# Summing the states of a Mamba scan on the four 64x64 tiles of TensorE

## The chip, the cores and the metric

One core of one Trainium2 chip runs the whole kernel in one launch. The metric is the device time in microseconds of one execution. Before the change it is 7373.88 us, the median of three runs (7371.5 to 7379.04).

## The reference, cut to what matters

The input x is (2, 256, 64, 64) in f32, seen as two sequences of 4096 tokens with 256 channels. Layer 0 is a group norm and a Mamba block with 256 inner channels. Layer 1 is a layer norm, a forward and a backward Mamba block with 512 inner channels each, and then a mixture of eight experts of three 256x256 layers. All five scan jobs share this recurrence over 16 states s, for every inner channel d and time t:

```
h[t,d,s] = exp(dt[t,d] * A[d,s]) * h[t-1,d,s] + dt[t,d] * xc[t,d] * B[t,s]
y[t,d]   = sum over s of h[t,d,s] * C[t,s]  +  xc[t,d] * D[d]
out      = (y * silu(z)) @ W_out
```

xc is a causal convolution of four taps of one half of the input projection, put through SiLU; z is the other half; dt is a softplus of a projection of xc; B and C are projections of xc too.

## The kernel before, in words

Channels lie on the 128 partitions and time on the free axis, in chunks of T = 512. Six jobs (layer 0, layer 1 forward and backward, for two batches) of eight chunks give 48 steps. A step has two blocks of 128 channels in layer 0 and four in layer 1. Blocks are taken in pairs (jp), so a layer-0 step has one pair and a layer-1 step two, 80 pairs in all. For each pair the 16 states are taken two at a time: a "quad" (i, jp, n) is two states by two blocks, 8 quads per pair (QN), 640 in all.

What a quad does, with the functions and lines that the change and the prediction's steps touch:

- SyncE loads the rows of B and of C for its two states, copied over all partitions (`load_bc`, L485 to L489). `want` and `flush` (L491 to L497) keep one list of loads for both kinds, in order; a load whose chunk has no B and C yet holds up those behind it.
- GpSimdE (POOL) multiplies dt * xc by B into a buffer bq, 128x2048 (`emit_b`, L504 to L516). There are six such buffers. At n = 0 it first makes xdt = dt * xc (L509).
- ScalarE (ACT) writes the decay exp(dt * A) into PSUM (`emit_decay`, L518), 128x512 at a time. There are two such PSUM tiles, each for one state and two blocks.
- VectorE (DVE) scans (`emit_scan`, L529), 128x512 at a time, four times per quad. In quads with even n the scan writes into bq, in those with odd n into the decay's tile.
- The product with C: for even n it is one POOL instruction of 128x2048 (`emit_times_c_quad`, L559), after a small ACT copy of the last column has saved the carry of the scan (`emit_carry`, L551). For odd n it is a DVE instruction of 128x1024 for each state, with a small DVE copy for the carry (`emit_times_c`, L541).
- TensorE (PE) sums over the states in PSUM by multiplying with an identity (`emit_sum`, L565): for each state and block one f32 matmul of a 128x128 identity with 128x512 of bq, into `y[:, j, :]`. The sum opens with a diagonal matmul for the D skip (`emit_skip`, L574). There is one y tile, of two PSUM banks. `emit_gate` (L583) on DVE multiplies y with silu(z), after which the next pair's skip can begin.

The order of the work around this is written by hand. For every step a `Slots` table holds the side work by slot and queue ("sp", "pe", "act", "dve", "pool"): `prepare` (L337) puts in the next step's projections xs and z, convolution, x_proj, softplus and gate, `norm` (L235) the layer norm, `finish` (L587) the output projection of the step before. A slot is one state of one quad; the main loop (L676 to L727) runs each slot's side work per queue and the slot's own work between it. In it, L693 to L704 say when a quad is summed, and L717 to L722 that POOL gets, in every other quad, the C product of the quad before and then two B products, for two and three quads ahead. The Tile framework then orders the instructions by its own scheduler within each engine, and adds the semaphores.

After the scans a second part computes the experts (L743 to L880). It isn't touched.

## Time and profile before

| | |
|---|---|
| median of three runs | 7373.88 us |
| profiled execution | 7371.24 us |
| its span, first to last instruction | 7369.5 us |
| mean granted TensorE clock | 0.909 |
| busy: PE / DVE / ACT / POOL | 6102.4 / 4677.5 / 3559.7 / 4535.2 us |
| sum over states, L569 (PE) | 5120 matmul instructions, 2363.6 us busy |
| B products, L511 (POOL) | 640 of 4523 ns |
| C products, L560 (POOL) | 320 of 4524 ns |
| C products, L546 (DVE) | 640 of 1218 ns |
| scans, L535 (DVE) | 2560 of 1207 to 1280 ns |
| table loads (ACT) | 416 of 1283 ns |

The profile shows one execution. Busy time is the time in which an engine has an instruction running. PE is the multiplying part of TensorE and PEld its weight loading, which lies beside it; an f32 matmul appears as two of each. For every wait, the profile names the engine and line that released it. A row of groups has the line, engine, operation, output and inputs, shapes, count, busy time, mean duration in ns, and after the bar the idle time just before them and what ended most of it. A row of a timeline has start, duration, engine, line and operation, and in brackets the idle time before it; several alike in a row are merged (x4). A row of the waits has who waited for whom, the total in us, how many times, and the longest.

### The profile page before, as it was taken

How to read it: one execution, taken by the hardware profiler on the slowest of the kernel's cores; microseconds unless marked ns; L12 is line 12 of the kernel's file. 1: busy time of each engine (PE TensorE's matmuls, PEld its weight loads, DVE VectorE, ACT ScalarE, POOL GpSimd, SP SyncE). 2: the span in 40 equal slices, each digit the busy share in tenths (PEclk: the TensorE clock that was granted, in tenths of full speed). 3: DMA queues.
4: the chain of work that ended last, by engine and by line, in shares of the span. 5: the costliest groups of instructions: out<-in, count | busy, mean ns of one | idle time of the engine just before them, and what ended most of it. 6: DMA issues, size and time to landing. Idle time of an engine off the chain costs nothing.

```text
span 7369.5 us, 43337 instructions
## 1 busy us (share of the span) xinstructions
PE 6102.4 (83%) x13160; PEld 2613.7 (35%) x13160; DVE 4677.5 (63%) x4889; ACT 3559.7 (48%) x5295; POOL 4535.2 (62%) x1062
## 2 busy tenths in 40 slices
PE   6888778878787888877777778777776999999999
PEld 2333333333333333333333333333333444444444
DVE  6889877778877877877787777787784111111111
ACT  7887556455445555544544544544542222222222
POOL 6889878878878878877887887887883000000000
PEclk8999989999999999988989889888887999999999
DMA  5444434434433443443343343343332000000000
GB/s 187 147 155 167 157 132 158 143 132 140 144 128 132 146 138 129 146 143 129 129 143 124 132 140 123 126 145 125 128 132 94 8 4 12 12 12 12 12 1 11
DMA packets 254189, 806.30 MB, mean 109 GB/s; under 512 B 26362, under 2 KB 35330, under 8 KB 253954
## 3 DMA queue, kind: packets, MB, share of 16 engines
q1 hardware_dynamic: 253954, 803.53, 32.6%
q8 instruction: 103, 1.69, 0.1%
q14 instruction: 132, 1.08, 0.0%
HBM read 749.95 MB, written 53.48 MB: 109 GB/s over the span
## 4 chain that ended last, share of the span: by engine, by line
POOL 27%; PE 22%; issue 16%; DVE 2%; ACT 1%; DMA 1%; POOLq 0%; SPq 0%; DVEq 0%; ACTq 0%
POOL bq L511 19%; PE hp L835 13%; POOL bq L560 7%; PE ym L869 6%; PE wb L860 1%; POOL xdt L509 1%; PE lg L805 1%; PE var_m L125 1%; DVE bq L535 1%; DVE da L535 1%; PE ym L855 0%; DMA t_dram<-xr 0%; ACT L108 0%; DVE cen_m L118 0%; DMA xr<-t_dram 0%
## 5 line engine op out<-in xcount | busy, mean ns | idle before, releaser
L511 POOL TENSOR_TENSOR bq<-xdt,bc 128x2048 f32<-128x2048 f32 x640 | 2880.7, 4523 | 555.0 <-PE y L569 553.4
L524 ACT ACTIVATE da<-dt,w_a 128x512 f32<-128x512 f32 x2564 | 1751.9, 689 | 1965.6 <-DVE h_state L549 1010.4
L569 PE MATMUL y<-bq,ident 128*128 128x512 f32 x5120 | 2363.6, 608 | 88.1 <-POOL bq L560 51.2
L535 DVE TENSOR_TENSOR_SCAN bq<-da,h_state,bq 128x512 f32<-128x512 f32 x1120 | 1360.0, 1267 | 631.9 <-POOL bq L511 605.2
L560 POOL TENSOR_TENSOR bq<-bq,bc 128x2048 f32<-128x2048 f32 x320 | 1447.6, 4524 | 311.8 <-ACT h_state L555 305.8
L569 PEld LDWEIGHTS y<-bq,ident 128*128 128x128 f32 x5120 | 1002.4, 197 | 1397.3 <-issue 1262.0
L535 DVE TENSOR_TENSOR_SCAN da<-da,h_state,bq 128x512 f32<-128x512 f32 x1120 | 1410.7, 1280 | 61.2 <-ACT da L524 31.4
L839 ACT ACTIVATE h<-hp,of,sc 128x512 f32<-128x512 f32 x512 | 398.4, 778 | 1024.1 <-PE hp L835 1024.1
L361 PE MATMUL conv<-xs,w_conv 128*128 128x512 f32 x1280 | 681.0, 682 | 249.0 <-ACT xs L351 248.1
L546 DVE TENSOR_TENSOR bq<-da,bc 128x1024 f32<-128x1024 f32 x640 | 778.8, 1218 | 12.7
L578 PE MATMUL y<-xc,w_d 128*128 128x512 f32 x320 | 275.0, 1009 | 541.2 <-DVE sz L585 541.2
L866 DVE TENSOR_TENSOR h<-h,wbs 128x1024 f32<-128x1024 f32 x128 | 156.9, 1226 | 874.7 <-ACT h L839 874.7
L361 PEld LDWEIGHTS conv<-xs,w_conv 128*128 128x128 f32 x1280 | 273.8, 219 | 641.5 <-issue 333.8
L835 PE MATMUL hp<-n,W 128*128 128x512 f32 x1024 | 490.4, 633 | 0.0
L835 PE MATMUL hp<-h,W 128*128 128x512 f32 x1024 | 449.9, 592 | 0.0
L869 PE MATMUL ym<-h,Wo 128*128 128x512 f32 x1024 | 449.9, 592 | 0.0
L326 PE MATMUL z<-nx,w_in 128*128 128x512 f32 x640 | 321.6, 635 | 133.4 <-DVE sz L444 76.7
L578 PEld LDWEIGHTS y<-xc,w_d 128*128 128x128 f32 x320 | 88.7, 303 | 680.5 <-DVE sz L585 599.7
L326 PE MATMUL xs<-nx,w_in 128*128 128x512 f32 x640 | 302.5, 604 | 15.0 <-DVE sz L444 5.9
L600 PE MATMUL o<-sz,w_out 128*128 128x512 f32 x640 | 311.9, 624 | 1.1 <-DVE sz L444 0.8
L835 PEld LDWEIGHTS hp<-n,W 128*128 128x128 f32 x1024 | 200.9, 202 | 293.4 <-issue 293.4
L509 POOL TENSOR_TENSOR xdt<-dt,xc 128x1024 f32<-128x1024 f32 x80 | 188.4, 2355 | 187.8 <-DVE dt L423 165.1
(121 smaller groups left out, 4424.2 us busy)
## 6 DMA issues: line engine op xcount, KB each, us to landing
bc<-bcd SPq DMA_DIRECT2D x1280, 512.0 KB, 3.9
t_dram<-xr SPq DMA_DIRECT2D x48, 512.0 KB, 3.6
x<-t_dram SPq DMA_DIRECT2D x32, 512.0 KB, 5.7
xr<-t_dram SPq DMA_DIRECT2D x32, 512.0 KB, 5.2
x<-in_x SPq DMA_DIRECT2D x16, 512.0 KB, 5.1
xr<-in_x SPq DMA_DIRECT2D x16, 512.0 KB, 3.8
t_dram<-x SPq DMA_DIRECT2D x16, 512.0 KB, 3.1
n_dram<-nx SPq DMA_DIRECT2D x16, 512.0 KB, 4.0
```

The source lines that it names most:

```text
L326: nc.tensor.matmul(ps, job.w["in"][:, k, m * P : (m + 1) * P], rhs, start=(k == 0), stop=(k == KC - 1),)
L361: nc.tensor.matmul(v["ps"], w["conv"][:, j, k, :], job.xs[:, j, k : k + T], start=(k == 0), stop=(k == 3),)
L511: nc.gpsimd.tensor_tensor(bq[g], ck["xdt", jp].rearrange("p (o j) t -> p o j t", o=1).to_broadcast([P, 2, 2, T]), bt.pop(g).rearrange("p s ...
L524: nc.scalar.activation(da[g, s][:, j, :], cks[i]["dt", jp][:, j, :], AF.Exp, scale=steps[i][0].w["a"][:, 2 * jp + j, 2 * n + s : 2 * n + s ...
L535: nc.vector.tensor_tensor_scan(d[:, j, :] if n % 2 else b, d[:, j, :], b, job.h[:, 2 * n + s, 2 * jp + j : 2 * jp + j + 1] if c else 0.0, ...
L546: nc.vector.tensor_tensor(bq[g][:, s, :, :], d, ct[g][:, s : s + 1, :].to_broadcast([P, 2, T]), ALU.mult)
L560: nc.gpsimd.tensor_tensor(bq[g], bq[g], ct[g].rearrange("p s (o t) -> p s o t", o=1).to_broadcast([P, 2, 2, T]), ALU.mult,)
L569: nc.tensor.matmul(y[i, jp][:, j, :], ident, bq[g][:, s, j, :], start=False, stop=(n == QN - 2 and s == 1),)
L578: nc.tensor.matmul(y[i, jp][:, j, :], job.w["d"][:, 2 * jp + j, :], cks[i]["xc", jp][:, j, :], start=True, stop=False,)
L835: nc.tensor.matmul(ps, w[:, k, m * P : (m + 1) * P], x[:, k, :], start=(k == 0), stop=(k == KC - 1),)
L839: nc.scalar.activation(h[:, m, :], ps, AF.Relu, bias=of[:, l, e, m : m + 1], scale=sc[:, l, e, m : m + 1],)
L869: nc.tensor.matmul(y[:, b, m, :], we["Wo", e][:, k, m * P : (m + 1) * P], h2[b][:, k, :], start=False, stop=(e == E - 1 and k == KC - 1),)
```

## The change

`emit_sum` and `emit_skip` no longer multiply with the full 128x128 array. They issue four matmuls instead of two, each with a 64x64 piece of the (diagonal) weight: the tile (r, col) takes rows 64r to 64r+63 of block j = (col - r) mod 2, and writes to partitions 64col to 64col+63 of bank r of y. So y holds the two blocks in another arrangement of channels than before. The host arranges the z columns of W_in and the rows of W_out alike (`summed`, `z_last`), so that gate and output projection fit.

The products with C on POOL are those of quads 0, 2, 3 and 5 instead of 0, 2, 4 and 6 (`POOL_C`, with the quad at which each is summed). The last quad of a pair is therefore one of DVE's. `POOL_AT` writes out at which quad POOL gets which C product (c) and B product (b). Loads of B and of C have a list each. DVE's side work runs between the two scans of a slot instead of before them. The layer norm's steps from the square on come one slot later, and in layer 1 the preparation of the next step starts at slot 4 instead of 5.

```diff
+TILES = [(r, col, (col - r) % 2) for r, col in ((0, 0), (1, 1), (0, 1), (1, 0))]
+POOL_C = {0: 2, 2: 4, 3: 5, 5: 7}
+POOL_AT = {0: "b3", 1: "c0 b4 b5", 3: "c2 b6", 4: "c3 b7", 6: "c5 b8 b9", 7: "b10"}
...
-                (0, "pe", mean), (1, "dve", centre), (1, "act", square), (2, "pe", variance),
-                (3, "act", roots), (4, "dve", divide), (4, "pool", add), (5, "act", affine),
-                (6, "sp", store),
+                (0, "pe", mean), (1, "dve", centre), (2, "act", square), (3, "pe", variance),
+                (4, "act", roots), (5, "dve", divide), (6, "pool", add), (6, "act", affine),
+                (7, "sp", store),
...
-                s0 += 5 if steps[i + 1][0].layer and not steps[i + 1][0].flip else 1
+                s0 += 6 if steps[i + 1][0].layer and not steps[i + 1][0].flip else 1
...
-        loads, wanted = [], []
+        loads, wanted = ([], []), []
...
         def want(h, *gs):
-            loads.extend((h, g) for g in gs if g < nq)
+            loads[h].extend(g for g in gs if g < nq)
 
         def flush():
-            while loads and "bc" in cks[quads[loads[0][1]][0]]:
-                h, g = loads.pop(0)
-                load_bc(g, h, ct if h else bt)
+            for h in range(2):
+                while loads[h] and "bc" in cks[quads[loads[h][0]][0]]:
+                    load_bc(loads[h].pop(0), h, ct if h else bt)
...
-        def emit_scan(g, s):
+        def emit_scan(g, s, j):
...
-            for j in range(2):
-                b = bq[g][:, s, j, :]
-                nc.vector.tensor_tensor_scan(
-                    d[:, j, :] if n % 2 else b, d[:, j, :], b,
...
+            b = bq[g][:, s, j, :]
+            nc.vector.tensor_tensor_scan(
+                b if n in POOL_C else d[:, j, :], d[:, j, :], b,
...
         def emit_sum(g, ss):
             i, jp, n = quads[g]
             for s in ss:
-                for j in range(2):
+                for r, col, j in TILES:
+                    rows, out_ = slice(64 * r, 64 * r + 64), slice(64 * col, 64 * col + 64)
                     nc.tensor.matmul(
-                        y[i, jp][:, j, :], ident, bq[g][:, s, j, :], start=False,
-                        stop=(n == QN - 2 and s == 1),
+                        y[i, jp][out_, r, :], ident[rows, rows], bq[g][rows, s, j, :],
+                        start=False, stop=(n == QN - 1 and s == 1),
                     )
...
-            for j in range(2):
+            for r, col, j in TILES:
+                rows, out_ = slice(64 * r, 64 * r + 64), slice(64 * col, 64 * col + 64)
                 nc.tensor.matmul(
-                    y[i, jp][:, j, :], job.w["d"][:, 2 * jp + j, :], cks[i]["xc", jp][:, j, :],
-                    start=True, stop=False,
+                    y[i, jp][out_, r, :], job.w["d"][rows, 2 * jp + j, rows],
+                    cks[i]["xc", jp][rows, j, :], start=True, stop=False,
                 )
...
-        want(0, 3, 4)
+        want(0, 3, 4, 5)
...
-                prepare(i + 1, 5 if wide else 0, sl, 1 if wide or steps[i + 1][0].nj == 2 else 2)
+                prepare(i + 1, 4 if wide else 0, sl, 1 if wide or steps[i + 1][0].nj == 2 else 2)
...
-                    sl.run(slot, "dve")
...
                     if s == 0:
-                        if n % 2 == 0:
-                            if g >= 1:
-                                emit_sum(g - 1, (1,))
-                            if g >= 2:
-                                emit_sum(g - 2, (0, 1))
...
-                    elif n % 2:
+                        if g and (n - 1) % QN not in POOL_C:
+                            emit_sum(g - 1, (1,))
+                        for m, due in POOL_C.items():
+                            if due == n:
+                                emit_sum(g - n + m, (0, 1))
+                    elif n not in POOL_C:
                         emit_sum(g, (0,))
...
-                    if s == 0 and n % 2:
+                    if s == 0 and n - 1 in POOL_C:
                         emit_carry(g - 1)
...
-                    if s == 0 and n % 2:
-                        emit_times_c_quad(g - 1)
-                        want_b(g + 2, g + 3)
-                        want(1, g + 1, g + 2)
-                        want(0, g + 4, g + 5)
+                    if s == 0:
+                        for what in POOL_AT.get(n, "").split():
+                            m = g - n + int(what[1:])
+                            if what[0] == "c":
+                                emit_times_c_quad(m)
+                            else:
+                                want(0, m + 3)
+                                flush()
+                                want_b(m)
+                    else:
+                        want(1, g + 2)
                         flush()
                     sl.run(slot, "pool")
 
-                    emit_scan(g, s)
-                    if n % 2:
+                    emit_scan(g, s, 0)
+                    sl.run(slot, "dve")
+                    emit_scan(g, s, 1)
+                    if n not in POOL_C:
                         emit_times_c(g, s)
...
+    def summed(din):
+        o = np.empty(din, np.int64)
+        for jp in range(din // (2 * P)):
+            for r, col, j in TILES:
+                at, of = (2 * jp + r) * P + 64 * col, (2 * jp + j) * P + 64 * r
+                o[at : at + 64] = np.arange(of, of + 64)
+        return o
+
+    def z_last(w):
+        din = w.shape[1] // 2
+        return np.concatenate([w[:, :din], w[:, din:][:, summed(din)]], axis=1)
```

## The prediction

> **What bounds the kernel now.** I read the windows first, to split the span, then the waits of the scan part, the timelines of two engines over one stall, and the groups.
>
> The window table (columns PE, weight loads, DVE, ACT, POOL busy, then clock and DMA), for the part with 512 inner channels and for the part after the scans:
>
> ```profile
> 1190.00:5605.00 4415.00, 3499.29 (x7374) 1484.98 (x7375) 3448.94 (x3566) 2216.43 (x3468) 3567.41 (x831) 0.90 0.40 134
> 5605.00:7369.50 1764.50, 1642.81 (x3756) 728.12 (x3754) 268.33 (x290) 487.07 (x612) 0.00 (x0) 0.92 0.04 14
> ```
>
> In the scan part three engines are each busy for 78 to 81%: none is full, they wait for each other. The change touches nothing in the last 1764.5 us (93% TensorE). The part before 1190 (L0, 16 pairs of blocks) has POOL at 965.0 of 1138 us. The waits of 1190 to 5605:
>
> ```profile
> DVE bq L535 <- POOL bq L511: 647.4, 232, 7.5
> ...
> POOL bq L511 <- PE y L569: 553.4, 85, 10.1
> ...
> POOL bq L560 <- ACT h_state L555: 270.9, 186, 5.2
> ...
> DVE xc L375 <- ACT thx L371: 201.5, 92, 3.3
> ```
>
> The scans wait for POOL's B product, and POOL's B product waits for TensorE to have summed the quad whose buffer it takes (six buffers bq). All 553.4 us of that wait of the whole run lie here. One such stall, on POOL and then on PE:
>
> ```profile
> 3028.21 8.98 POOL L511 TENSOR_TENSOR bq<-xdt,bc 128x2048 f32<-128x2048 f32 x2 [7.63 <-PE y L569]
> ```
>
> ```profile
> 3022.81 1.88 PE L569 MATMUL y<-bq,ident 128*128 128x512 f32 x4
> 3024.53 1.88 PE L326 MATMUL xs<-nx,w_in 128*128 128x512 f32 x4
> 3026.24 5.31 PE L569 MATMUL y<-bq,ident 128*128 128x512 f32 x12
> 3031.39 3.60 PE L361 MATMUL conv<-xs,w_conv 128*128 128x512 f32 x8
> ```
>
> PE is not waiting here: it works off a queue without a gap, and the sum that frees the buffer is in its turn at 3026. So TensorE binds where a chunk's projections and convolutions fall, and the cost lands on POOL, then on DVE. How much of TensorE the sums are:
>
> ```profile
> L569 PE MATMUL y<-bq,ident 128*128 128x512 f32 x5120 | 2363.6, 608 | 88.1 <-POOL bq L560 51.2
> ```
>
> 5120 instructions for 640 x 2 x 2 = 2560 calls: an f32 matmul is two load-and-multiply passes, and in the timeline passes start 0.43 us apart (12 in 5.31 with the last lasting 0.59).
>
> **What the Trainium skill says.** "TensorEngine Tiling (Array Packing)", Key Properties: tiles work independently and may load and multiply in parallel, and a change of tiling mode drains TensorE. The trace of before has no 64x64 form, but it has a mode change, priced below. Same page, Restrictions and Gotchas: different row tiles must not use one PSUM bank at a time; the change writes row half r to bank r of y, so this rule is kept (no run here shows the price of breaking it). "TensorE: Matmul & The Clock Gate", Part 3, Measured speedup: sixteen 32x32 tiles gave 10.6 times; whether in f32 is not said, and no run here shows it. Same part, The mechanism: matmuls start and end in program order; before agrees as far as it goes, one tile's passes follow each other at 0.43 us.
>
> **The change, part by part.**
>
> *Sums and skip.* 2560 + 160 calls become 5120 + 320, each with a 64x64 weight and all 512 columns, so each pass streams as long as now, 0.43 us. One state of a quad is 4 tile calls, 8 passes. Four tiles at once: two rounds, 0.86 us. Now: 2 calls, 4 passes, 1.72 us. So full overlap halves 2363.6 to 1182 us, one running at a time doubles it to 4727; I take full overlap because the skill states independence and a measured gain, and keep both ends. Weight loads double to 8 per state: the trace has two loads in 0.29 us with 0.18 for one, so 0.11 apart, 8 x 0.11 = 0.85 us, just under 0.86 if a 64-column load costs as much as one of 128. It should not bind.
>
> *Mode changes.* The instruction order of the changed kernel has 1257 changes between tiled and full matmuls, 16 per pair of blocks. Price from before, where an 8-row weight comes between full ones:
>
> ```profile
> 6344.77 4.03 PE L869 MATMUL ym<-h,Wo 128*128 128x512 f32 x9
> 6348.73 1.12 PE L860 MATMUL wb<-wts,sel 8*128 8x512 f32 x2
> 6349.78 3.70 PE L835 MATMUL hp<-n,W 128*128 128x512 f32 x8
> ```
>
> The last L869 pass starts 0.59 before its end, 6348.21; the second pass of L835 starts at about 6350.31. That is 2.10 us for four passes, against 4 x 0.43 = 1.72: 0.38 for two changes, 0.19 each. 1257 x 0.19 = 239 us of TensorE, about 3 per pair. Lower bound nothing, upper twice that.
>
> *TensorE in sum, 1190 to 5605.* 3499 busy now; 4060 of the 5120 sum passes lie here with 1848 us, skip 234. Halved: -924 and about -55 (half of 252 x 0.43), plus changes 63 pairs x 3 = 190: 2710 of 4415 us. Its idle time covers the changes. If overlap fails the cover is gone (rivals).
>
> *Where the stall goes.* POOL's 553.4 us on PE go. Next late is what then sets POOL and DVE: POOL without this wait is 4415 - 553 = 3862 (3567 busy, 271 behind the carry copy); DVE without its POOL wait is 4415 - 647 = 3768. So 3862 is left, not less, unless the carry wait shrinks too.
>
> *C products to quads 0, 2, 3, 5.* Four POOL products of 4.52 and four DVE pairs of 1.22 per pair of blocks, as now: no busy time. The order is new. Laid out by hand: DVE takes 4.9 us for a POOL quad (4 scans at an effective 1.23) and 7.6 for a DVE quad, 54.7 per pair with the rest (3449/63); POOL 56.6 (3567/63). c0 stands before b4, b5; c2 before b6; c3 before b7; c5 before xdt, b8 and b9. POOL waits at c2 and c5 for at most some 2 us, then runs behind DVE and waits no more; each B product is ready 5 us or more before its scans. Each slot that a B product takes is nominally summed one quad earlier, as now. Quad 7 ends on DVE, so the sum closes without a POOL product behind it. I take nothing for gain or loss; bounds -150 (half the carry wait) and +150.
>
> *Two load lists, DVE side work between two scans, layer-norm one slot later, preparation one slot earlier.* Same 1280 loads, same DVE instructions; a load lands in 3.9 us and is asked for 1.5 or more quads (over 10 us) ahead: nothing.
>
> *ACT.* The order moves its softplus apart: 517 table loads instead of 416, 101 x 1.283 = 130 us. ACT has half its time idle, but the four softplus stand in consecutive slots, each before a decay that a scan waits for. Between 0 and 130; I take 65.
>
> *Host permutation* of W_out and the z columns: no device time.
>
> Sum: 7371.2 (profiled execution, 7369.5 span + 1.7; 2.6 under the median 7373.9) - 553 + 65 + about 20 for waits that reappear (TensorE still stops for up to 6 us at conv for ACT's xs, 240 us in all) = **6900**. With the carry wait halved as well and no table cost: about 6670. With half of the PE wait left: about 7150.
>
> **Rivals.**
>
> *The passes queue (7450).* If tile calls start in program order, a tile's second pass waits for its first, and the next tile's first stands behind it: one call per 0.43 us, 4 x 0.43 = 1.72 per state, as now. TensorE gains nothing and pays 239 us of mode changes. For: program order as the skill has it, passes at 0.43 in before. Against: independence, and the rows alternate from call to call. PE at 3499 + 190 of 4415 keeps its queue; a third of the changes lands: 7371 + 80. Order effects: 7200 to 7650.
>
> *The tiles take turns (9400), the slower side.* Place: TensorE's queue at the sums. Price: 2364 for sums, 136 for skip, 239 for changes: 2739 us more. PE's idle before 5605 is 916 + 203 = 1119; some 400 of it (waits for xs and for the gate) stays. So 2739 - 719 = 2020 lands: about 9400. It decides once the sums cost over about 1.25 times now (4415 - 3499 - 190, less 250 of stays, over 1848). For: no f32 tile is shown anywhere. Against: the skill's measured gain.
>
> *TensorE is freed but ACT and DVE take its place (7250).* With POOL no longer holding it up, DVE comes sooner to what ACT makes: all 130 of the table loads land, the wait for thx (201) doubles, that for da (44) grows by 100: 7371 - 553 + 130 + 201 + 100 = 7250. For: thx is the largest DVE wait that is not POOL's. Against: ACT is busy for only 2216 of 4415 us.
>
> **How the numbers follow.** Forecast 0.54, queueing 0.20, turns 0.18, ACT and DVE 0.08. A measurement of this kernel tells about 0.2% from no change, 7359 to 7389. Faster: 0.54 + 0.04 (queueing, below it) + 0.04 = 0.62; same 0.02 + 0.03 = 0.05; slower 0.14 + 0.18 + 0.01 = 0.33. The range reaches from 6620 to 7650, over the forecast and two rivals; it leaves out the turns and the tails of the others, some 0.2. Forecast's own range: 6650 to 7150.
>
> **What would show it.** Right: the 64x64 rows of the sum start four to a pass time; PE busy falls from 6102 to about 5100; POOL's wait on PE y falls below 100 us; ACT shows 517 table loads with DVE's waits on ACT little longer. Queueing: tile calls one per 0.43 us, PE busy unchanged or up. Turns: 0.86 us per call, PE over 90% before the sums end. If POOL's wait is gone and the time is not, a DVE wait on ACT must have grown.

## The result, and the profile after

| | before | changed |
|---|---|---|
| median | 7373.19 us (7371.5 to 7379.04) | 7913.18 us (7911.66 to 7916.12, four runs) |
| ratio | | 1.0731, 95% interval 1.0713 to 1.075 |
| span of the profiled run, granted clock | 7369.5 us, 0.909 | 7914.2 us, 0.826 |

The changed kernel is 540 us slower; the forecast was 6900, with a range from 6620 to 7650. The line of busy times on the changed kernel's page:

```profile
PE 5416.3 (68%) x18600; PEld 1941.3 (25%) x18600; DVE 4662.9 (59%) x4889; ACT 3672.0 (46%) x5392; POOL 4532.9 (57%) x1062
```

TensorE has 686 us less to do than before (6102.4). ScalarE has 112 us more (the table loads), VectorE and GpSimd have what they had. No engine is busy for more than 68% of the span, so the 540 us are waiting. The window of the changed kernel for the part with 512 inner channels (columns as in the prediction):

```profile
1240.00:6140.00 4900.00, 2923.49 (x11580) 940.85 (x11572) 3399.14 (x3533) 2320.64 (x3541) 3532.95 (x824) 0.78 0.35 120
```

The scan part went from 4415 to 4900 us, and the granted clock in it from 0.90 to 0.78 while TensorE stands idle for longer. The part after the scans is as it was, but for 10 us (1774 against 1764.5). Three groups of the changed kernel:

```profile
L518 POOL TENSOR_TENSOR bq<-xdt,bc 128x2048 f32<-128x2048 f32 x640 | 2878.3, 4517 | 534.7 <-PE y L576 522.6
L566 POOL TENSOR_TENSOR bq<-bq,bc 128x2048 f32<-128x2048 f32 x320 | 1446.3, 4522 | 863.1 <-ACT h_state L561 838.0
...
L576 PE MATMUL y<-bq,ident 64*64 64x512 f32 x10240 | 1409.7, 646 | 137.4 <-POOL bq L566 69.7
```

The sums take 1409.7 us instead of 2363.6, so the tiles do overlap. Yet POOL's wait for the sums, which was to go, is still 522.6 us (before 553.4), and POOL's C products now wait 838.0 us for the small ScalarE copy that saves the carry (before 305.8). The waits of the changed kernel's scan part, by who waits for whom:

```profile
ACT da L531 <- DVE h_state L555: 1442.6, 344, 13.8
PE y L586 <- DVE sz L593: 849.2, 63, 23.6
...
DVE da L541 <- POOL bq L518: 597.2, 98, 9.4
...
PE dbc L394 <- DVE xc L382: 383.0, 30, 12.8
PE conv L368 <- ACT xs L358: 350.9, 30, 13.3
```

Every engine waits for another, and the longest single waits in these lines are 9 to 24 us, where a quad takes 9.7 us in the mean (4900 us for 63 pairs of 8). One of these stalls in the timeline of the changed kernel, four engines in order of time:

```profile
3081.74 4.52 POOL L566 TENSOR_TENSOR bq<-bq,bc 128x2048 f32<-128x2048 f32 x1 [4.26 <-ACT h_state L561]
...
3082.92 0.58 ACT L358 COPY xs<-xs 128x512 f32<-128x512 f32 x1
...
3085.54 1.88 PE L333 MATMUL xs<-nx,w_in 128*128 128x512 f32 x4
3086.22 8.96 POOL L518 TENSOR_TENSOR bq<-xdt,bc 128x2048 f32<-128x2048 f32 x2
3087.35 1.07 PE L576 MATMUL y<-bq,ident 64*64 64x512 f32 x2
3090.75 4.82 DVE L541 TENSOR_TENSOR_SCAN da<-da,h_state,bq 128x512 f32<-128x512 f32 x4 [9.37 <-POOL bq L518]
...
3096.78 2.02 ACT L531 ACTIVATE da<-dt,w_a 128x512 f32<-128x512 f32 x3 [13.29 <-DVE h_state L555]
...
3100.54 0.57 ACT L358 COPY xs<-xs 128x512 f32<-128x512 f32 x1
...
3101.16 5.81 PE L368 MATMUL conv<-xs,w_conv 128*128 128x512 f32 x8 [12.74 <-ACT xs L358]
...
3106.90 1.94 PE L576 MATMUL y<-bq,ident 64*64 64x512 f32 x14
...
3108.94 4.51 POOL L518 TENSOR_TENSOR bq<-xdt,bc 128x2048 f32<-128x2048 f32 x1 [13.77 <-PE y L576]
```

Read it backwards. At 3108.94 POOL has waited 13.77 us for a sum. That sum stood in TensorE's queue behind a convolution, which waited 12.74 us for ScalarE to copy out the projection xs finished at 3087.4. (It doesn't read that projection but the one of the block before, copied at 3082.92; what it needs is the PSUM tile, as e5 below confirms.) ScalarE came to that copy at 3100.54, because decays stood ahead of it in its queue, and the first of them waited 13.29 us for VectorE to free a decay tile. VectorE had waited 9.37 us for a B product of POOL, and POOL came to that product at 3086.22, after a C product for whose carry copy it had waited 4.26 us. POOL, TensorE, ScalarE and VectorE wait for each other in a ring, and none of them is short of capacity in it. This is one stall; the experiments are to tell which link of the ring counts.

### The profile page after: what moved, and what is told of

Same layout as the page of the kernel before. It is cut to its first block, busy times and chain, and to the rows that moved or that the text cites. A ratio compares the mean times of both kernels' runs of the same rounds, so it can differ in the third digit from the quotient of the medians.

```text
span 7914.2 us, 54386 instructions
## 1 busy us (share of the span) xinstructions
PE 5416.3 (68%) x18600; PEld 1941.3 (25%) x18600; DVE 4662.9 (59%) x4889; ACT 3672.0 (46%) x5392; POOL 4532.9 (57%) x1062
## 4 chain that ended last, share of the span: by engine, by line
POOL 33%; issue 31%; PE 21%; DVE 6%; ACT 3%; DMA 1%; SPq 0%; POOLq 0%; DVEq 0%; ACTq 0%
POOL bq L518 25%; PE hp L846 12%; POOL bq L566 7%; PE ym L880 6%; DVE da L541 2%; POOL xdt L516 2%; DVE bq L541 1%; ACT da L531 1%; PE wb L871 1%; DMA bc<-bcd 1%; DVE bq L552 1%; PE lg L816 1%; PE var_m L132 1%; PE ym L866 0%; ACT L115 0%
## 5 line engine op out<-in xcount | busy, mean ns | idle before, releaser
L518 POOL TENSOR_TENSOR bq<-xdt,bc 128x2048 f32<-128x2048 f32 x640 | 2878.3, 4517 | 534.7 <-PE y L576 522.6
L566 POOL TENSOR_TENSOR bq<-bq,bc 128x2048 f32<-128x2048 f32 x320 | 1446.3, 4522 | 863.1 <-ACT h_state L561 838.0
L576 PE MATMUL y<-bq,ident 64*64 64x512 f32 x10240 | 1409.7, 646 | 137.4 <-POOL bq L566 69.7
L368 PE MATMUL conv<-xs,w_conv 128*128 128x512 f32 x1280 | 658.2, 662 | 392.6 <-ACT xs L358 392.5
L586 PE MATMUL y<-xc,w_d 64*64 64x512 f32 x640 | 195.1, 975 | 858.0 <-DVE sz L593 858.0
L576 PEld LDWEIGHTS y<-bq,ident 64*64 64x64 f32 x10240 | 380.1, 144 | 1172.2 <-issue 933.6
L333 PE MATMUL z<-nx,w_in 128*128 128x512 f32 x640 | 410.4, 785 | 310.7 <-DVE sz L451 122.7
L394 PE MATMUL dbc<-xc,w_x 128*128 128x512 f32 x320 | 201.7, 760 | 459.0 <-DVE xc L382 397.6
L333 PE MATMUL xs<-nx,w_in 128*128 128x512 f32 x640 | 330.8, 642 | 78.4 <-DVE sz L451 41.8
L608 PE MATMUL o<-sz,w_out 128*128 128x512 f32 x640 | 351.7, 687 | 20.9 <-DVE xc L382 19.7
L333 PEld LDWEIGHTS z<-nx,w_in 128*128 128x128 f32 x640 | 142.3, 241 | 554.3 <-DVE sz L451 157.7
```

The source lines that it names most:

```text
L333: nc.tensor.matmul(ps, job.w["in"][:, k, m * P : (m + 1) * P], rhs, start=(k == 0), stop=(k == KC - 1),)
L368: nc.tensor.matmul(v["ps"], w["conv"][:, j, k, :], job.xs[:, j, k : k + T], start=(k == 0), stop=(k == 3),)
L518: nc.gpsimd.tensor_tensor(bq[g], ck["xdt", jp].rearrange("p (o j) t -> p o j t", o=1).to_broadcast([P, 2, 2, T]), bt.pop(g).rearrange("p s ...
L566: nc.gpsimd.tensor_tensor(bq[g], bq[g], ct[g].rearrange("p s (o t) -> p s o t", o=1).to_broadcast([P, 2, 2, T]), ALU.mult,)
L576: nc.tensor.matmul(y[i, jp][out_, r, :], ident[rows, rows], bq[g][rows, s, j, :], start=False, stop=(n == QN - 1 and s == 1),)
L608: nc.tensor.matmul(v[m], job.w["out"][:, j, m * P : (m + 1) * P], ck["sz", j // 2][:, j % 2, :], start=(j == 0), stop=(j == job.nj - 1),)
```

## The experiments

Three theories stood at the start, after the built order of GpSimd's work was read (the order in which the Tile scheduler, "the builder" below, leaves an engine's instructions). It is not the one that the prediction laid out. As written, a pair of blocks runs b0 b1 b2 b3 c0 b4 b5 c2 b6 c3 b7 c5 (b and c with the quad's number). As built, the pairs differ; the most frequent order, in 19 of 80, is "b0 c0 b1 b2 c2 b3 b4 c3 b5 b6 c5 b7", and in 48 of 80 c0 stands ahead of b2: a C product, which waits for the scan just done, stands ahead of the B product for the next scan. Theory A says that this order is the loss, and that the tiles gain. Theory B says that TensorE loses by changes of mode or the lower clock. Theory C blames the rest of the new schedule: ScalarE's table loads, the place of the layer norm and of VectorE's side work. The ratios below are to runs of the kernel before made beside each set, 7371 to 7381 us.

### Tiles and schedule apart

**e1**, the kernel before with tiles in sum and skip alone:

```diff
-                for j in range(2):
+                for r, col, j in TILES:
+                    rows, out_ = slice(64 * r, 64 * r + 64), slice(64 * col, 64 * col + 64)
...
-                        y[i, jp][:, j, :], ident, bq[g][:, s, j, :], start=False,
+                        y[i, jp][out_, r, :], ident[rows, rows], bq[g][rows, s, j, :], start=False,
```

> The kernel before with only the sum and the skip on 64x64 tiles (and the channels arranged for it); the order on POOL is built as before. Theory A (the loss lies in the built order on POOL, where a C product comes ahead of the next B product; the tiles themselves gain): POOL's wait on the sums falls from 553 us to under 200, time 6950 to 7200. Theory B (the loss lies in TensorE: mode changes and a lower granted clock): time 7600 to 8000. Theory C (ACT's table loads, the place of layer norm and of DVE's side work): time 6900 to 7200, as for A.

Measured: 7439.8 us, ratio 1.008 (1.0064 to 1.0097). None of the theories has it. The group of sums in this run, and then two of its waits:

```profile
L571 PE MATMUL y<-bq,ident 64*64 64x512 f32 x10240 | 1434.8, 641 | 138.9 <-POOL bq L561 71.4
```

```profile
POOL bq L512 <- PE y L571: 529.1, 71, 11.1
...
PE conv L362 <- ACT xs L352: 348.7, 68, 11.7
```

TensorE is rid of 929 us of sums (661 us of all its work, since other passes got slower), and nothing comes of it: POOL waits for the sums about as long as before (553.4), and TensorE's own wait at the convolution grew from 248.1. TensorE's throughput did not bind. Where the 61 us more come from stays open.

**e2**, the changed kernel with full-array sums and skip (the diff of e1 taken back):

> The changed kernel with its sums and skips on the full array again; the built order on POOL has the C product ahead of the next B product as in the changed kernel. Theory A: at least as slow as the changed kernel, 7900 to 8200, since the same POOL order now also waits for the slower sums. Theory B: the loss is gone, 7300 to 7450. Theory C: slow as for A, 7800 to 8200.

Measured: 7933.74 us, ratio 1.075 (1.0734 to 1.0766), carry wait 830.0. The loss is in the new schedule as built, with tiles (7913) and without; e2 has no changes of mode, and B, which had 7300 to 7450 for it, is out.

**e3** and **e4**, the changed kernel and the kernel before, with GpSimd's instructions held in program order (`keep_in_program_order` makes the Tile scheduler leave them in the order in which the program issues them):

```diff
+    keep = tc.keep_in_program_order
...
-            nc.gpsimd.tensor_tensor(
+            keep(nc.gpsimd.tensor_tensor(
```

> The changed kernel with POOL's instructions held in the order in which the source writes them (b0 b1 b2 b3 c0 b4 b5 c2 b6 c3 b7 c5); nothing else changed. Theory A: POOL's wait for the carry falls from 838 to under 350 us and DVE's wait for B products from 1197 to under 600; time 6750 to 7000. Theory B: 7600 to 7900. Theory C: 7500 to 7800, with DVE waits on ACT in place of those on POOL.

> The kernel before with POOL's instructions held in the order of its source (one B product more ahead of each C product). Theory A: the order matters only where the sums free their buffers in time; with sums on the full array the B products that are asked for earlier wait on TensorE instead: 7200 to 7450. Theories B and C say nothing of it: 7370.

Measured: e3 7572.12 us, ratio 1.026 (1.0245 to 1.0276); e4 7526.84, ratio 1.0198 (1.0183 to 1.0213). Three waits of e3:

```profile
POOL bq L519 <- PE y L577: 940.1, 141, 11.2
PE y L587 <- DVE sz L594: 930.0, 65, 20.6
...
POOL bq L567 <- ACT h_state L562: 38.3, 10, 7.6
```

The carry's wait is nearly gone (838.0 before), as A has it, and 341 of the 540 us with it; A's time, 6750 to 7000, was missed by far. VectorE's wait for B products fell from 1197 to 863 us, where A had under 600. C's range, 7500 to 7800, holds the time, but VectorE's waits on ScalarE in the scans, which C had in POOL's place, grew by only 46 us (426 to 472). The wait for the sums rose to 940.1 instead. Most of it comes behind another stall than the one shown above: in the trace, TensorE's longest idle time within 8 us ahead of or in POOL's wait is that of the skip for VectorE's gate (the 930.0 above) for 59 of the 141 waits and 434 us, and that of the x_proj matmuls (dbc) for VectorE's xc for 31 waits and 342 us. And e4, which missed A's 7200 to 7450, shows that holding GpSimd in the written order is no gain in itself. A holds for a part.

### The wait at the convolution

The ring suggested taking the convolution's wait away. **e5** (from before) and **e6** (from e1) let it read an operand that is ready:

```diff
-                            v["ps"], w["conv"][:, j, k, :], job.xs[:, j, k : k + T],
+                            v["ps"], w["conv"][:, j, k, :], ck["nx"][:, k % KC, :],
```

> The kernel before, with one operand changed: the convolution's matmuls read the normed tokens (nx) in place of the copied projection xs, so TensorE no longer waits there for ScalarE's copy; the copy itself stays. (The convolution's result is left wrong by that; the instructions and GpSimd's order are those of before.) Ring theory (TensorE's queue is in order, so a sum stands behind a convolution that waits for ScalarE, GpSimd's next B product waits for the sum, VectorE for the B product, ScalarE's decay for VectorE): GpSimd's wait for the sums falls from 555 us to below 300, and the time to 7080-7280. Throughput theory (TensorE's 6209 us of work are the limit): the backlog stays, GpSimd's wait for the sums stays above 450, the time falls by at most the 248 us that TensorE waited, half of it likely: 7200-7340. Rival that another engine (VectorE with 5280 us in hand) sets the pace: 7340-7400.

> The kernel before with sums and skip on four tiles, and with the same changed operand of the convolution (it reads nx; its result is left wrong by that). Ring theory: what the tiles save was swallowed by the wait at the convolution (349 us in the run with tiles alone); without it GpSimd's wait for the sums falls from 529 to below 200, the time to 6950-7200, and it lies 50-250 us below the kernel with the full-array sums and the same operand. Rival that mode changes and the lower granted clock eat the tiles' gain: it lies 0-1.5% above that kernel again, as tiles alone lay 0.8% above the kernel before. Rival that VectorE sets the pace: 7340-7450, no gain at all.

Measured: e5 7379.94 us, ratio 0.9997 (0.9988 to 1.0006); e6 7430.63, ratio 1.0064 (1.0049 to 1.0079). The wait at the convolution in e5:

```profile
PE conv L361 <- ACT xs L351: 247.7, 66, 5.6
```

The wait is still there with the same releaser, though nothing is read from that copy any more. So it is not for the data. The side matmuls share two PSUM tiles (pool psp), and the convolution needs the one that ScalarE's copy empties. The edit took no wait away and tests no theory, though e5's time lies in the range of its last rival; it says which resource closes the ring. (TensorE's work before is 6102.4 us; the 6209 in e5's text is that of e2.)

### Other orders on TensorE and GpSimd, another buffer

**e7** and **e8** write a slot's side matmuls behind its sums and hold TensorE and GpSimd in program order; e8 with full-array sums:

```diff
-                    sl.run(slot, "pe")
                     if s == 0:
                         if g and (n - 1) % QN not in POOL_C:
...
                         emit_sum(g, (0,))
+                    sl.run(slot, "pe")
...
-                    nc.tensor.matmul(
+                    keep(nc.tensor.matmul(
```

> The changed kernel with the order of TensorE and GpSimd held as the program writes it, and with a slot's side matmuls written behind its sums instead of ahead of them. Ring theory: GpSimd's wait for the sums falls from 940 us (GpSimd's order alone held) to below 400, the carry's wait stays small, and the time is 6900-7250. Rival that only the order on GpSimd counted and the rest is set by GpSimd's own 4533 us in the chain with VectorE: 7450-7600, as with GpSimd's order alone (7572). Rival that TensorE held in order loses what the scheduler had won by mixing: above 7600, with TensorE waiting longer at the side matmuls.

> The same as the run before in this list, with full-array sums and skip in place of the tiles: what the tiles are worth in this order. Ring theory: with GpSimd's wait on the sums loosened TensorE is the next limit, so it is slower than with tiles by 100-400 us: 7100-7600. Rival that the tiles are worth nothing (mode changes, lower clock): within 1% of the kernel with tiles.

Measured: e7 7595.93 us, ratio 1.029 (1.0274 to 1.0305); e8 7806.3, ratio 1.0573 (1.0557 to 1.0588). The convolution's wait fell to 55 us, the wait for the sums was still 621.0 with tiles and 913.5 without. So the wait at the convolution is not the lever by itself. The side work was late elsewhere, and on VectorE: the projection z waited 363 us for it to empty a PSUM tile (sz), the projection dt 263 us. The ring theory's 6900 to 7250 was missed; the time is about that of GpSimd held alone (e3). The tiles are worth 210 us here.

**e9** and **e10** write GpSimd's order anew, with one B product ahead of each C product; e10 with full-array sums:

```diff
-POOL_AT = {0: "b3", 1: "c0 b4 b5", 3: "c2 b6", 4: "c3 b7", 6: "c5 b8 b9", 7: "b10"}
+POOL_AT = {0: "b1", 1: "c0 b2", 2: "b3", 3: "c2 b4", 4: "c3 b5", 5: "b6", 6: "c5 b7", 7: "b8"}
...
-        want(0, 3, 4, 5)
+        want(0, 3)
         flush()
-        want_b(0, 1, 2)
+        want_b(0)
```

> The changed kernel with GpSimd held in program order, and that order rewritten so that exactly one B product stands ahead of each C product (b0 b1 c0 b2 b3 c2 b4 c3 b5 b6 c5 b7), as in the kernel before. Theory that both orders failed by their distance (the built one by none ahead: carry's wait 838 us; the written one by three ahead, which keeps all six buffers full: 940 us of waiting for sums): both waits fall under 500 us and the time to 7250-7450. Rival that the written order was as good as any and the ring through the side matmuls sets the rest: 7520-7620, as the written order's 7572. Rival that VectorE now starves for B products: 7650-7900.

> The same order on GpSimd with full-array sums and skip. If TensorE's time counts in this order, it is slower than with tiles by 100-400 us (7400-7800); if the tiles are worth nothing, as they were in the order of before, it lies within 1% of the kernel with tiles.

Measured: e9 7790.59 us, ratio 1.0558 (1.0542 to 1.0573); e10 7888.02, ratio 1.0688 (1.0672 to 1.0704). The theory of distance, 7250 to 7450, was missed. The time is in the range of the rival by which VectorE starves for B products, but VectorE waited 1072.8 us for them, less than in the changed kernel (1197), so that rival does not explain the loss. The tiles are worth 97 us here, where 100 to 400 were expected.

**e11** gives e3 a seventh product buffer:

```diff
-        bcp = st.enter_context(tc.tile_pool(name="bcp", bufs=4))
+        bcp = st.enter_context(tc.tile_pool(name="bcp", bufs=3))
...
-        bqp = st.enter_context(tc.tile_pool(name="bqp", bufs=6))
+        bqp = st.enter_context(tc.tile_pool(name="bqp", bufs=7))
```

> The changed kernel with GpSimd held in the order as written and seven product buffers in place of six (and three row buffers of each kind in place of four, for the room). Buffer theory: GpSimd's wait for the sums (940 us with six) is a wait for a free buffer and falls below 600; time 7250-7480. Rival that the wait is TensorE's lateness in a ring, which a buffer only moves: the wait stays above 800 and the time at 7520-7620. Mishap that speaks for neither: GpSimd waits over 150 us for the rows' loads.

Measured: 7696.9 us, ratio 1.0424 (1.0407 to 1.0442), slower than e3, with 908.3 us of waiting for the sums. A seventh buffer did not help; the fewer row buffers are not to blame (0.9 us of waiting for the rows), but the builder also put ScalarE's side work further back (table below), so buffers alone were not varied. No order on GpSimd and no buffer repaired it.

### ScalarE's order

**e12** is e9 with ScalarE held in program order too, and a slot's side work on ScalarE written ahead of its decays:

```diff
+                    sl.run(slot, "act")
                     if s == 0:
                         emit_decay(g, 1)
                     else:
                         emit_decay(g + 1, 0)
-                    sl.run(slot, "act")
...
-                nc.scalar.activation(
+                keep(nc.scalar.activation(
```

> As the first kernel of this list, and ScalarE's side work (its copies of the projection, tanh and the rest) stands ahead of the decays of a slot, ScalarE held in program order. Ring theory: the wait of the convolution's matmuls for ScalarE's copy frees a PSUM buffer sooner: that wait falls below 150 us, and the time is 50-250 us under the first kernel's. Rival that the decays now come late: VectorE waits over 300 us more for ScalarE, and the time is 50-300 us above.

Measured: 7262.52 us, ratio 0.9839 (0.9824 to 0.9853): 528 us under e9, where the ring theory asked for 50 to 250. The waits of e12 that tell:

```profile
POOL bq L567 <- ACT h_state L562: 810.3, 240, 10.2
...
PE conv L369 <- ACT xs L359: 12.7, 12, 3.5
```

POOL's wait for the sums is not in the list any more. The link at which the ring opened is ScalarE's order, with what the builder made of it on the other engines. Two things were changed at once, the place of the side work and the holding of it. So the next four runs, all with GpSimd and ScalarE held and the tiles unless said otherwise: **e13**, GpSimd's order as written (the POOL_AT of the changed kernel), side work first; **e14**, the same with full-array sums; **e15**, two B products ahead; **e16**, both orders as the changed kernel writes them, decays first. The edit of e15 against e12 (e13 has the table of the changed kernel at this place, and e14 the diff of e1 taken back besides):

```diff
-POOL_AT = {0: "b1", 1: "c0 b2", 2: "b3", 3: "c2 b4", 4: "c3 b5", 5: "b6", 6: "c5 b7", 7: "b8"}
+POOL_AT = {0: "b2", 1: "c0 b3", 2: "b4", 3: "c2 b5", 4: "c3 b6", 5: "b7", 6: "c5 b8", 7: "b9"}
...
-        want(0, 3)
+        want(0, 3, 4)
...
-        want_b(0)
+        want_b(0, 1)
```

and of e16 against the changed kernel:

```diff
-            nc.gpsimd.tensor_tensor(
+            keep(nc.gpsimd.tensor_tensor(
...
-                nc.scalar.activation(
+                keep(nc.scalar.activation(
```

> The changed kernel with GpSimd held in the order as written (up to three B products ahead of a C product) and ScalarE held with its side work ahead of a slot's decays. In the run with one B product ahead and the copies first, GpSimd's wait for sums was gone and its wait for the carry was 810 us: the C products came too close behind their scans. Theory: with more distance the carry's wait falls below 300, the sums' wait stays below 300, and the time is 6950-7200. Rival that the six buffers fill up again: the sums' wait comes back with over 500 us and the time is 7300-7600.

> The same with full-array sums and skip: what the tiles are worth once nothing on ScalarE holds TensorE up. Theory that TensorE's work counts only then: slower than with tiles by 100-500 us. Rival that the tiles are worth nothing in any order: within 1% of the kernel with tiles.

> With tiles and the copies first, two B products ahead of each C product (b0 b1 b2 c0 b3 b4 c2 b5 c3 b6 b7 c5): between the order as written and the one with one ahead. Theory: the carry's wait under 500, time 7000-7230, within 100 us of the order as written. Rival that distance doesn't matter once the copies are first: within 0.5% of 7262.

> The changed kernel with GpSimd and ScalarE both held in the order as written, decays ahead of the side work. It tells the order of ScalarE's work apart from the holding of it. Ring theory: the ring is as it was with GpSimd alone held (7572): 7480-7750, the sums' wait above 700. Rival that any fixed order on ScalarE gains: 7000-7350.

Measured: e13 7007.28 us, ratio 0.9505 (0.9491 to 0.952); e14 7148.96, ratio 0.9697 (0.9681 to 0.9713); e15 7015.31, ratio 0.9517 (0.9503 to 0.9531); e16 6874.59, ratio 0.9327 (0.9313 to 0.9341). The times of e13, e14 and e15 were as expected, but the carry's waits of e13 and e15 were not (565 and 610 us, where under 300 and under 500 were asked for). e16 is the best of them, and the ring theory expected nothing of it (7480 to 7750): the place ahead of the decays is no gain but costs 133 us against the place behind them (e13 against e16). It is the holding that gained. e3 and e16 are the same program but for the holding of ScalarE, and have GpSimd in the same order; they differ by 0.093 of the time of before, some 690 us. Three of e16's waits:

```profile
POOL bq L567 <- ACT h_state L562: 456.7, 125, 12.0
...
PE y L587 <- DVE sz L594: 321.4, 69, 8.5
...
PE conv L369 <- ACT xs L359: 29.9, 13, 6.3
```

What the builder does to ScalarE can be counted in the lists of built instructions. In program order, the tanh of a convolution (thx) has no decay ahead of it that is written behind it. In the built order of the changed kernel it has 14 (median over 160), in before 14 too, in e1 to e6, e9 and e10 14, in e7 and e8 16, in e11 18; in e12 to e18 none. Fourteen decays are seven slots, three and a half quads. The decays can't run ahead in fact, since there are two tiles for them; so whatever stands behind them waits for VectorE. TensorE's order, by contrast, is the same in the median in e3 and e16. VectorE's is not: with ScalarE held, the builder also puts VectorE's side work earlier. In the traces xc has 10 scans more ahead of it in e3 than in e16 (median), dt 12, sz 10 and the gate 13, and the changed kernel stands much as e3, e17 as e16. TensorE's wait of the skip for that gate falls from 930.0 to 321.4 us. So what the holding removed is the lateness of the side work on ScalarE and on VectorE together; no run has the one without the other.

**e17** holds ScalarE alone in the changed kernel, **e18** is e16 with full-array sums:

```diff
+    keep = tc.keep_in_program_order
...
-                    nc.scalar.copy(job.xs[:, j, 3:], ps[0])
+                    keep(nc.scalar.copy(job.xs[:, j, 3:], ps[0]))
...
-                nc.scalar.activation(
+                keep(nc.scalar.activation(
```

> The changed kernel with ScalarE alone held in the order as written; GpSimd's order is the builder's. With both held the time was 6875, with GpSimd alone 7572, with neither 7913. In the built order ScalarE's side work stands 12 to 14 decays later than the program has it, and the convolution and dbc matmuls wait for it. Theory that this lateness is the main cause: 6880-7250, and GpSimd's wait for the sums below 200 us. Rival that both orders must be held: 7400-7800.

> The changed kernel with GpSimd and ScalarE held in the order as written (6875 with tiles), and full-array sums and skip. It says what the tiles are worth in the best order so far. From the pair with the copies first (7149 against 7007) they are worth some 140 us: 6970-7150. Rival that they are worth nothing here: within 0.5% of 6875. If TensorE's work were the limit as forecast, more than 400 us: above 7275.

Measured: e17 6868.7 us, ratio 0.9307 (0.9293 to 0.932); e18 7034.72, ratio 0.9529 (0.9514 to 0.9545). Holding ScalarE alone turns 7913 into 6869, 511 us under before, and it is the fastest kernel of this study. GpSimd's order in e17 is again the builder's, which makes another one than in the changed kernel (c0 behind b5 in 63 of 80 pairs, c5 mostly in the next pair). With that order and with the written one (e16) the time is the same within 0.2% (ratios 0.9307 and 0.9327). The windows of e17, scan part, and then of e18:

```profile
1240.00:5092.00 3852.00, 2861.20 (x11596) 888.65 (x11598) 3444.10 (x3557) 2363.20 (x3576) 3552.08 (x829) 0.87 0.47 154
```

```profile
1240.00:5259.00 4019.00, 3416.89 (x7316) 1440.50 (x7314) 3445.86 (x3557) 2362.79 (x3576) 3556.14 (x830) 0.93 0.45 147
```

In e17 POOL is busy for 3552 of 3852 us (92%), and it is now the engine nearest to its limit; in e18 it is 88%. The waits of e17's scan part:

```profile
POOL bq L567 <- ACT h_state L562: 273.6, 85, 7.8
...
POOL bq L519 <- PE y L577: 2.3, 10, 0.4
```

POOL's wait for the sums is 2.3 us. TensorE's timeline in e17 where a chunk's convolutions fall:

```profile
2989.75 1.09 PE L577 MATMUL y<-bq,ident 64*64 64x512 f32 x8
2990.77 3.70 PE L369 MATMUL conv<-xs,w_conv 128*128 128x512 f32 x8
2994.40 2.81 PE L577 MATMUL y<-bq,ident 64*64 64x512 f32 x24
2997.14 3.70 PE L369 MATMUL conv<-xs,w_conv 128*128 128x512 f32 x8
```

Sums and side matmuls alternate without a gap; in the stall of the changed kernel shown above a gap of 12.74 us stood ahead of a convolution.

### All runs in one table

Waits in us over the whole run; the last column counts the decays that stand ahead of a tanh against program order (median).

| run | time | POOL for sums | POOL for carry | decays ahead |
|---|---|---|---|---|
| before | 7373 | 553 | 306 | 14 |
| changed | 7913 | 523 | 838 | 14 |
| e1 tiles alone | 7440 | 529 | 353 | 14 |
| e2 schedule alone | 7934 | 556 | 830 | 14 |
| e3 POOL held | 7572 | 940 | 38 | 14 |
| e4 before, POOL held | 7527 | 561 | 71 | 14 |
| e5 before, conv reads nx | 7380 | 563 | 304 | 14 |
| e6 e1, conv reads nx | 7431 | 550 | 360 | 14 |
| e7 POOL and PE held, side matmuls last | 7596 | 621 | 50 | 16 |
| e8 e7 without tiles | 7806 | 914 | 42 | 16 |
| e9 one ahead | 7791 | 556 | 277 | 14 |
| e10 e9 without tiles | 7888 | 655 | 260 | 14 |
| e11 seventh buffer | 7697 | 908 | 41 | 18 |
| e12 e9, ACT held, side work first | 7263 | 0 | 810 | 0 |
| e13 written, ACT held, side work first | 7007 | 0 | 565 | 0 |
| e14 e13 without tiles | 7149 | 0 | 753 | 0 |
| e15 two ahead, ACT held, side work first | 7015 | 0 | 610 | 0 |
| e16 written, POOL and ACT held | 6875 | 0 | 457 | 0 |
| e17 ACT held alone | 6869 | 13 | 325 | 0 |
| e18 e16 without tiles | 7035 | 0 | 635 | 0 |

## Why the prediction was wrong

The forecast was faster by 474 us; the change is slower by 540. Its steps, in turn:

- *Tiles overlap fully, sums halve to 1182 us: right.* 24 passes of a tile form take 2.81 us in e17, the last of them 0.59: six rounds of four, 0.43 us apart. Busy time of the sums in the changed kernel is 1409.7 us and not 1182, since some of them trickle in and some run slow after an idle stretch (last section).
- *Mode changes, 0.19 us each: about right.* It was priced at an 8-row weight, but the lines of e17 above have it for the tiles: eight convolution passes take 3.63 us from their start to that of the tiles behind them, 0.19 more than 8 x 0.43; 24 tile passes take 2.74, 0.16 more than 6 x 0.43. In sum, e16 against e18: TensorE's busy time falls by 691 us, that of sum and skip by 1022, so the rest grew by 331; over the 1296 changes in e16's trace that is at most 0.26 us each, since slow passes after an idle stretch are in it.
- *"PE is not waiting here: it works off a queue without a gap ... So TensorE binds": this step failed.* The lines shown there began too late. Six microseconds earlier, before's own timeline has

```profile
3013.38 1.42 ACT L524 ACTIVATE da<-dt,w_a 128x512 f32<-128x512 f32 x2 [2.48 <-DVE bq L535]
...
3016.51 0.58 ACT L351 COPY xs<-xs 128x512 f32<-128x512 f32 x1
...
3017.14 5.83 PE L361 MATMUL conv<-xs,w_conv 128*128 128x512 f32 x8 [5.04 <-ACT xs L351]
```

  TensorE had stood for 5.04 us at a convolution, and was working off what that had dammed up. Faster sums clear the dam sooner but don't end the wait for ScalarE; e1 shows it, 929 us less of sums and 61 us more of time. The prediction knew the 240 us at the convolution and priced them as a leftover of about 20. They were the dam: in the trace of before, TensorE's longest idle time within 8 us ahead of or in POOL's wait is at a convolution for 61 of the 85 waits, 518 of the 553 us. What keeps such dams up is the late side work (in e7 the wait at the convolution is down to 55 us, and others stand in its place).
- *"Where the stall goes. POOL's 553.4 us on PE go": failed with it.* It stayed at 522.6, and went to 13 only when ScalarE's order was held.
- *"The order is new. Laid out by hand ... I take nothing for gain or loss; bounds -150 and +150": failed, in size and sign.* The layout was read from the program, and the builder makes another order of it, on GpSimd, on ScalarE and on VectorE. The new schedule in the builder's order cost 555 us (e2 against before); with GpSimd and ScalarE as written it lies 345 us under before (e18). For the program as written the layout was right in one half: in e16 POOL's wait for the sums vanishes. In the other it was not: by it POOL "waits no more", and in e16 POOL waits 456.7 us for the carry copies.
- *ACT, 517 table loads for 65 us: the count was right,* the cost is not to be seen apart. VectorE's wait for the softplus grew from 55 to 121 us, but e17 has 523 loads and is the fastest, so they are not the loss.
- *The rivals.* Queueing and turns are out by the sums' busy time. "ACT and DVE take its place" named the right engines, with a different mechanism (POOL's wait gone, and more work on ScalarE) and a chance of 0.08.
- *Two side sums are loose:* by their own terms "about 6670" comes to some 6690 and "about 7150" to some 7180. Nothing hangs on them.

That e17 lands at 6869, close to the forecast of 6900, does not make the sum right. It came by another way: of the 0.067 by which e16 is faster than before, the tiles give 0.020 (e16 against e18), some 150 us, not the 553 of the wait that they were to end. The other 0.047 comes with the new schedule and the held orders together.

What stays open. Which part of the new schedule makes it more sensitive to late side work, when before has the same 14 decays ahead and loses less, is known only for GpSimd's order (341 of 540 us, e3); the earlier preparation, the later layer norm and the side work between the scans were not tried alone. The kernel before with ScalarE held in program order was not tried, so the 345 us of e18 are not divided between schedule and holding. Whether it is the place of the side work on ScalarE or on VectorE that counts is not shown either: e3 and e16 differ in both, e17 and the changed kernel in GpSimd's order as well. Holding VectorE alone would tell.

## What to carry to other kernels

When an engine's queue seems full at a stall, go back along it until it last stood idle, and ask for what: the work seen after that is what the idle time dammed up, and making it faster moved nothing here (e1). Where a scheduler reorders the program, read the built order of every engine, not of the one that the change is about alone; here the side work of ScalarE and VectorE stood late, in queues that the prediction did not read. When a wait names data that can be had at once, look at the buffer that its releaser empties.

## What the runs showed of the hardware

Four 64x64 tiles in f32 run side by side at the full rate of one: in e17, at 2994.40, four passes start within 0.02 us of each other, each lasts 0.59 to 0.64 us as a pass of the full array does, and in a long group the next four follow 0.43 us later. The tiles' weight loads take 145 ns in the mean (e17), against 197 for 128x128 (before), and do not hold the passes up.

And a stall costs TensorE more than the stall: eight passes of the convolution take 3.60 us in a busy stretch of before (at 3031.39 in the prediction's lines), but 5.83 after 5.04 us of idling in before and 5.81 after 12.74 in the changed kernel. In both of these the granted clock is 0.50 for the first 3.8 us and passes start about 0.85 us apart, then 0.43. That agrees with the Trainium skill ("TensorE: Matmul & The Clock Gate", Part 1), by which the clock is halved once TensorE has been idle for about 3.4 us, and comes back after as long a busy time. The mean granted clock of the scan part goes with the share of busy time: 0.93 at 85% (e18), 0.87 at 74% (e17), 0.78 at 60% (the changed kernel). This mean counts idle time too, in which the granted clock also falls (0.63 in the 12.6 us ahead of the changed kernel's convolution), so it is not the clock at which the passes ran.
